# A two-layer adaLN kernel: the results of the last mixture of experts gathered one step ahead, their sums placed by hand on VectorE

## The chip, the cores and the metric

One core of one Trainium2 chip runs the whole kernel. The metric is the device time of one execution in microseconds (us); the time of a kernel is the median of its runs. A profile is one further execution, recorded instruction by instruction.

The engines are named as the profile names them: PE is the matrix engine (TensorE), DVE is VectorE, ACT is ScalarE, POOL is GpSimd, and SP only issues transfers. Each engine works through its own queue in order. An instruction that waits holds up everything queued behind it on its engine.

## The reference, cut to what matters

The kernel computes two transformer-like layers on 4096 tokens of width 128. Only the end of the second layer is touched: a mixture of eight experts with a top-2 choice, a capacity of 512 slots for each expert, and a residual sum.

```python
def _dispatch_compute(xf, top_expert, w1, w2, capacity):
    ...
    xe = jnp.where(valid[..., None], xf[tok_idx], 0.0)
    h = jax.nn.gelu(jnp.einsum('ech,ehf->ecf', xe, w1), approximate=True)
    ye = jnp.einsum('ecf,efh->ech', h, w2)
    ...
    out = jnp.zeros((tokens + 1, hs), xf.dtype).at[tok_safe.reshape(-1)].add(ye.reshape(-1, hs))
    return out[:tokens]
...
for k in range(TOP_K):
    y = _dispatch_compute(xf, top_experts[:, k].astype(jnp.int32), w1, w2, capacity)
    out = out + y * expert_weights[:, k][:, None]
return out.reshape(sl, bs, hs) + bias
...
x = x + gb * _L1_ffn_ref(h, L1_ffn_router_w, L1_ffn_w1, L1_ffn_w2, L1_ffn_bias)
```

There are 4096 tokens in this stage, so the capacity is 4096 / 8 = 512 slots for each expert and choice. What matters here is its last part: each token's two expert results are fetched, multiplied by a weight and by the gate `gb`, and added to `x`.

## The kernel before

The kernel is one program whose instructions are written in Python loops and then ordered by a planner. The planner simulates the engines while it places instructions: of the instructions that it takes to be ready it issues the one that was traced first, so the order on an engine can differ from the order of the text. `tc.keep_in_program_order(ins)` adds an edge that holds `ins` behind the last instruction traced on its engine before it; it is an order of issue and not a wait.

The end of the kernel has three stages.

**The slots stage.** `slots_steps` (L1312) runs over the two choices `k` and the eight experts `e`, 16 experts in all. `expert(k, e)` loads 512 rows of the expert's inputs (`xe`), transposes them on PE (`xtp`), copies them from PSUM on DVE (`xT`, L1272) and multiplies them with the first weights (`ph`, 8 matmul instructions) into ACT's gelu (`act`, L1278). `expert_out` (L1281) multiplies with the second weights (`ypy`, 32 instructions), copies the result on DVE (`ye`, L1290) and stores it from ACT's queue to `slots_out` in HBM (L1291). `expert_out` of one expert is traced after `expert` of the next. `outs` gives `ypy` two PSUM buffers; `xtp` has one.

**The gathers.** `collect(k, g)` (L1293) handles four tiles of 128 tokens. For each tile, POOL issues an indirect transfer (L1297) that gathers 128 rows of `slots_out` by an index list into a tile `y` (a ring of 8 buffers); DVE multiplies `y` by weight and gate (L1305) and adds it to `x` (L1308). 28 of the 32 tiles go this way, in 7 groups of four. For `k` = 0 the groups are traced in the slots stage, group `e` in the step of expert (1, `e`). A gather of choice `k` reads all of `slots_out[k]`, so it can start only when all eight experts' results of that choice have been stored. For `k` = 1 the groups are traced in the next stage, and SP stores each finished group (L1310).

**The blocks stage.** The last 512 tokens were sorted into 15 blocks of 128 rows with one expert each. `last_experts` (L1092) goes over them in pairs: `hidden(j)` does the first multiplication (`gph`) and the gelu (`gact`), at every second pair also the transpose (`gtp`) and DVE's copy of it (`gxT`, L1118); `results(j)` does the second multiplication (`gpy`, one PSUM buffer), DVE's product with the gate (`gye`, L1139), the next weights' loads on SP and a store to `g_out`. `results` of a pair is traced after `hidden` of the next pair. `Beside.take(1)` runs the generator by one pair. For each group `g` the loop takes one pair and then traces `collect(1, g)`; the eighth pair and the last `results` follow behind the seventh group.

**The tail.** `return_steps` gathers the last 512 tokens' rows from `g_out` (8 gathers `fy`, L287), adds them and stores.

Of the kernel before, what the change touches and what calls it, by code (L numbers as in the profile page):

```python
# [14 lines left out]
ALU = mybir.AluOpType  # L15
# [5 lines left out]
NT = B * S // P  # L21
TB = S // P
# [18 lines left out]
NL = TB // 2  # L41
# [3 lines left out]
def mm(nc, out, lhsT, rhs, start=True, stop=True):  # L45
    return nc.tensor.matmul(out, lhsT, rhs, start=start, stop=stop)  # L46
# [3 lines left out]
def adaln_two_layers(ctx: ExitStack, tc: tile.TileContext, I: dict, out: bass.AP):  # L50
    nc = tc.nc
# [43 lines left out]
    with tc.tile_pool(name="mw", bufs=1) as mw, tc.tile_pool(name="mps", bufs=2, space=PSUM) as mps:  # L95
        for l in range(2):
# [23 lines left out]
            for m in (2, 5):  # L120
# [7 lines left out]
                g = cst.tile([P, B, D], F32, name=f"gate{l}{m}")  # L128
                nc.vector.scalar_tensor_tensor(g, raw, -1.0, size, ALU.add, ALU.mult)
                gate.append(g)  # L130
    gate_a0, gate_b0, gate_a1, gate_b1 = gate
# [130 lines left out]
    def load_block(pool, bufs, tag, table, expert, j):  # L262

        w = pool.tile([P, I[table].shape[2]], F32, tag=tag, bufs=bufs, name=tag)

        with tc.issue_after(loads[-1].ins) if loads else nullcontext():
            e = nc.sync.value_load(expert[0:1, j : j + 1], min_val=0, max_val=NE - 1)
            loads.append(nc.sync.dma_start(w.unsqueeze(1), I[table][bass.ds(e, 1)].rearrange("e p c -> p e c")))
        return w
# [193 lines left out]
    with ExitStack() as es:  # L463
# [192 lines left out]
        blocks = None  # L656
# [4 lines left out]
        for at, (b, c) in enumerate(stages):  # L661
            q, k = made
# [45 lines left out]
            blocks = None  # L708
            if c == 0 and b > 0:
                blocks = Blocks(b - 1, ab, (ps_m, "m"), [(ps_m, "m")], rest)  # L710
# [20 lines left out]
    wgt = w1l.tile([P, 2, NT], F32, name="wgt")  # L731
# [5 lines left out]
    with ExitStack() as es:  # L737
# [354 lines left out]
        def last_experts():  # L1092

            b, nb = B - 1, NLB
            expert = sent[0][0]
            rows_in = g_in.rearrange("(q p) d -> p q d", p=P)
            rows_out = g_out.rearrange("(q p) d -> p q d", p=P)
            ws, ins, xT, ye = {}, {}, {}, {}

            def load(j):  # L1100
                for r in range(j, min(j + 2, nb)):
                    ws[r] = load_block(eb, 6, "gw", "g_w", expert, r)

            def rows(q):
                n = min(4, nb - q)
                ins[q] = eb.tile([P, 4, D], F32, tag="gxe", name="gxe")
                nc.sync.dma_start(ins[q][:, :n], rows_in[:, q : q + n])

            def hidden(j):
                q = j - j % 4  # L1110
                if j == q:
                    n = min(4, nb - q)
                    tp = ps_m.tile([P, 4, P], F32, tag="m", name="gtp")
                    for r in range(n):
                        nc.tensor.transpose(tp[:, r], ins[q][:, r], ident)
                    xT[q] = eb.tile([P, 4, P], F32, tag="gxT", name="gxT")
                    shift, scale = modT[1][:, 3, b : b + 1], modT[1][:, 4, b : b + 1]
                    nc.vector.tensor_scalar(xT[q][:, :n], tp[:, :n], scale, shift, ALU.mult, ALU.add)  # L1118
                    if q + 4 < nb:
                        rows(q + 4)  # L1120
                    ye[q] = eb.tile([P, 4, D], F32, tag="gye", name="gye")
                n = min(2, nb - j)
                ph = [ps_u.tile([P, NFC, P], F32, tag=f"pu{(j + r) % 4}", name="gph") for r in range(n)]
                act = eb.tile([P, 2, NFC, P], F32, tag="gact", name="gact")
                for r in range(n):
                    for f in range(NFC):
                        mm(nc, ph[r][:, f], ws[j + r][:, f * P : (f + 1) * P], xT[q][:, j - q + r])
                    nc.scalar.activation(act[:, r], ph[r], AF.Gelu_apprx_tanh)
                return j, n, act

            def results(j, n, act):
                q = j - j % 4
                py = ps_y.tile([P, 2, D], F32, tag="py", name="gpy")
                for r in range(n):
                    w = ws.pop(j + r)
                    for f in range(NFC):
                        w2 = w[:, NFC * P + f * D : NFC * P + (f + 1) * D]
                        mm(nc, py[:, r], act[:, r, f], w2, start=(f == 0), stop=(f == NFC - 1))
                nc.vector.tensor_mul(  # L1139
                    ye[q][:, j - q : j - q + n], py[:, :n], gate_b1[:, b : b + 1, :].to_broadcast([P, n, D])  # L1140
                )
                if j + 6 < nb:
                    load(j + 6)
                if j > q or j + n == nb:
                    nc.scalar.dma_start(rows_out[:, q : j + n], ye[q][:, : j + n - q])

            rows(0)
            for j in range(0, 6, 2):
                load(j)
            made = None  # L1150
            for j in range(0, nb, 2):
                ahead = hidden(j)
                if made is not None:
                    results(*made)
                made = ahead
                yield
            results(*made)
# [26 lines left out]
        for b in range(B):  # L1184
# [17 lines left out]
            for m in range(NCH):  # L1202

                g, n = divmod(m, NCH // 2)
# [56 lines left out]
        def expert(k, e):  # L1261
            at = slice(e * CAP, (e + 1) * CAP)
            xe = eb.tile([P, NS, D], F32, tag="xe", bufs=4, name="xe")
            load_xe = nc.sync.dma_start(xe, xd[k][at, :].rearrange("(q p) d -> p q d", p=P))
            if (k, e) == (1, NE - 1):

                loads.append(load_xe)
            tp = ps_m.tile([P, CAP], F32, tag="m", name="xtp")
            for q in range(NS):
                nc.tensor.transpose(tp[:, q * P : (q + 1) * P], xe[:, q, :], ident)  # L1270
            xT = eb.tile([P, CAP], F32, tag="xT", name="xT")
            nc.vector.tensor_copy(xT, tp)  # L1272
            act = eb.tile([P, NFC, CAP], F32, tag="act", name="act")
            for f in range(NFC):
                pool, tag = next(banks)
                ph = pool.tile([P, CAP], F32, tag=tag, name="ph")
                mm(nc, ph, g_w[:, e, f * P : (f + 1) * P], xT)
                nc.scalar.activation(act[:, f, :], ph, AF.Gelu_apprx_tanh)  # L1278
            return e, k, act

        def expert_out(e, k, act):  # L1281
            at = slice(e * CAP, (e + 1) * CAP)
            pool, tag = next(outs)
            py = pool.tile([P, NS, D], F32, tag=tag, name="ypy")
            for q in range(NS):
                for f in range(NFC):
                    w = g_w[:, e, NFC * P + f * D : NFC * P + (f + 1) * D]
                    mm(nc, py[:, q, :], act[:, f, q * P : (q + 1) * P], w, start=(f == 0), stop=(f == NFC - 1))
            ye = eb.tile([P, NS, D], F32, tag="ye", name="ye")
            nc.vector.tensor_copy(ye, py)  # L1290
            nc.scalar.dma_start(yd[k][at, :].rearrange("(q p) d -> p q d", p=P), ye)  # L1291

        def collect(k, g):  # L1293

            for t in range(4 * g, 4 * g + 4):
                y = eb.tile([P, D], F32, tag="y", bufs=8, name="y")
                nc.gpsimd.indirect_dma_start(  # L1297
                    out=y,
                    out_offset=None,
                    in_=yd[k][:, :],  # L1300
                    in_offset=bass.IndirectOffsetOnAxis(ap=slot[:, k, t : t + 1], axis=0),
                    bounds_check=NSLOT - 1,
                    oob_is_err=False,
                )
                nc.vector.scalar_tensor_tensor(  # L1305
                    y, y, wgt[:, k, t : t + 1], gate_b1[:, t // TB, :], ALU.mult, ALU.mult
                )
                nc.vector.tensor_add(x[:, t, :], x[:, t, :], y)  # L1308
            if k == 1:
                nc.sync.dma_start(outv[:, 4 * g : 4 * g + 4, :], x[:, 4 * g : 4 * g + 4, :])  # L1310

        def slots_steps():  # L1312
            waiting = None
            for k in range(2):
                for e in range(NE):
                    made = expert(k, e)
                    yield
                    if waiting is not None:
                        expert_out(*waiting)
                    waiting = made  # L1320
                    if k == 1 and 4 * e < NT - NL:
                        collect(0, e)
                    yield
            expert_out(*waiting)

# [4 lines left out]
            sending.take(sending.n)  # L1330
        slots.rest()
        blocks = Beside(last_experts(), 0, 1)
        for g in range((NT - NL) // 4):
            blocks.take(1)
            collect(1, g)
        blocks.rest()
        _, placei, w = sent[0]
        drained(return_steps(g_out, NT - NL, NL, placei, w, db, 6, store=True))
# [73 lines left out]
```

## Time and profile before

| | us |
|---|---|
| median of 3 runs | 2165.16 (2164.11 to 2168.03) |
| the profiled execution's own time | 2174.76 |
| its span, first to last instruction | 2173.1 |
| slots stage's second half, experts (1, 1) on: first `ph` | 2004.01 |
| first gather of choice 0 | 2007.76 |
| blocks stage: first `gph` | 2091.13 |
| first gather of choice 1 | 2095.02 |
| first gather of the tail | 2158.26 |

Busy shares over the whole span: PE 82%, DVE 61%, POOL 46%, ACT 44%. In the stretch from 2004 to 2057 us PE was busy 29.93 of 53 us, and from 2095 to 2158 us 31.63 of 63 us. The 56 gathers took POOL 994 to 1528 ns each, 996 in the median.

How to read the lines that follow in the prediction: a line of the timeline has the start in us, the busy time, the engine, the line of the kernel, the operation, the output and inputs, the shapes and the count; in brackets stands how long the engine sat idle before it and what ended that. A line of the waits has who waited, for whom, the total in us, the number of times and the longest. "remote" or "an unknown queue" means that the record doesn't tell what ended the wait. A line of the chain has the start, the length and the work or wait that the end hung on.

### The profile page before, as it was taken

How to read it: one execution, taken by the hardware profiler on the slowest of the kernel's cores; microseconds unless marked ns; L12 is line 12 of the kernel's file. 1: busy time of each engine (PE TensorE's matmuls, PEld its weight loads, DVE VectorE, ACT ScalarE, POOL GpSimd, SP SyncE). 2: the span in 40 equal slices, each digit the busy share in tenths (PEclk: the TensorE clock that was granted, in tenths of full speed). 3: DMA queues.
4: the chain of work that ended last, by engine and by line, in shares of the span. 5: the costliest groups of instructions: out<-in, count | busy, mean ns of one | idle time of the engine just before them, and what ended most of it. 6: DMA issues, size and time to landing. Idle time of an engine off the chain costs nothing. (4 is left out here: it accounts for less than half of the span.)

```text
span 2173.1 us, 29054 instructions
## 1 busy us (share of the span) xinstructions
PE 1790.6 (82%) x8957; PEld 967.9 (45%) x8957; DVE 1322.2 (61%) x4000; ACT 948.1 (44%) x2073; POOL 997.5 (46%) x1277
## 2 busy tenths in 40 slices
PE   5399999998999999899988899958688777659573
PEld 3144444454555344455534455523245323237363
DVE  5446566665667667566766566647678796941322
ACT  1145454653445375354365345544465354323111
POOL 1334534336423635532544533345563867740433
PEclk9699999999999999999999999988799877869786
DMA  6400101001222201222300122110122400012334
GB/s 224 128 1 19 31 1 34 16 19 45 67 71 70 64 1 41 66 69 64 83 13 24 51 71 66 52 37 0 36 65 79 144 9 20 15 60 82 115 94 127
DMA packets 103756, 123.59 MB, mean 57 GB/s; under 512 B 15024, under 2 KB 68656, under 8 KB 103600
## 3 DMA queue, kind: packets, MB, share of 16 engines
q1 hardware_dynamic: 84256, 99.01, 15.6%
q0 software_dynamic: 8192, 16.74, 2.6%
q10 hardware_dynamic: 11152, 5.97, 0.9%
q8 instruction: 71, 1.16, 0.2%
q14 instruction: 85, 0.70, 0.1%
HBM read 67.85 MB, written 32.90 MB: 46 GB/s over the span
## 5 line engine op out<-in xcount | busy, mean ns | idle before, releaser
L586 POOL TENSOR_SCALAR pr<-pr,den 128x32 f32<-128x32 f32 (+31 forms) x512 | 354.6, 709 | 303.4 <-DVE den L583 297.2
L580 ACT ACTIVATE pr<-pr,nb 128x32 f32<-128x32 f32 (+31 forms) x512 | 371.6, 727 | 197.3 <-DVE nb L567 193.0
L595 PE MATMUL pt<-ident,pr 128*128 128x128 f32 x2304 | 341.8, 283 | 47.1 <-POOL pr L586 37.6
L46 PE MATMUL sc<-k,q 64*128 64x512 f32 (+14 forms) x1536 | 332.7, 525 | 44.4 <-DVE nb L567 25.3
L595 PEld LDWEIGHTS pt<-ident,pr 128*128 128x128 f32 x2304 | 253.5, 142 | 244.0 <-POOL pr L586 78.8
L46 PE MATMUL po<-pT,v 128*64 128x512 f32 x1152 | 345.4, 621 | 1.9 <-DVE pT L599 1.5
L597 ACT COPY pT<-pt 128x512 f32<-128x512 f32 x288 | 167.8, 583 | 362.5 <-PE pt L595 297.7
L567 DVE CUSTOM_DVE_ANT_0 pr<-sc,mask 128x512 f32<-128x512 f32 (+15 forms) x512 | 273.0, 559 | 73.5 <-PE sc L46 64.1
L599 DVE COPY pT<-pt 128x512 f32<-128x512 f32 x288 | 198.3, 688 | 167.3 <-PE pt L595 153.7
L46 PEld LDWEIGHTS sc<-k,q 64*128 64x128 f32 x1536 | 123.8, 193 | 199.9 <-DVE nb L567 94.7
L914 POOL TENSOR_TENSOR hc<-h,cc 128x512 f32<-128x512 f32 x128 | 161.9, 1278 | 102.1 <-DVE h L910 37.7
L46 PE MATMUL pu<-du,spread 128*128 128x512 f32 x256 | 147.0, 679 | 48.8 <-DVE h L910 41.7
L684 POOL MEMSET pr<- 128x288 f32 x128 | 42.4, 340 | 262.8 <-PE pt L595 258.8
L567 DVE CUSTOM_DVE_ANT_0 pr<-sc,mask,nb 128x416 f32<-128x416 f32 (+15 forms) x256 | 119.9, 496 | 6.9 <-PE sc L46 5.8
L908 ACT ACTIVATE da<-dt,negA 128x512 f32<-128x512 f32 x128 | 91.6, 719 | 65.5 <-DVE h L910 65.1
L1297 POOL DMA_INDIRECT y<-slots_out,slot x56 | 56.9, 1016 | 126.6 <-issue 59.2
L46 PEld LDWEIGHTS po<-pT,v 128*64 128x64 f32 x1152 | 69.4, 135 | 84.9 <-issue 44.5
L503 DVE TENSOR_TENSOR rot_w<-proj,sin_sb 128x512 f32<-128x512 f32 x80 | 55.0, 688 | 79.8 <-PE proj L46 45.9
L906 DVE TENSOR_TENSOR pu<-pu,bb 128x512 f32<-128x512 f32 x128 | 85.1, 684 | 23.8 <-PE pu L46 23.3
L46 PEld LDWEIGHTS pu<-du,spread 128*128 128x128 f32 x256 | 45.8, 208 | 117.8 <-DVE h L910 70.5
L545 POOL TENSOR_TENSOR q<-rot_u,rot_v 128x512 f32<-128x512 f32 x64 | 81.3, 1272 | 35.1 <-DMA rot_v<-rot_w 26.2
L580 ACT ACTIVATION_READ_ACCUMULATOR pr<-pr,nb 128x1 f32 x512 | 96.3, 188 | 0.0
(273 smaller groups left out, 2708.9 us busy)
## 6 DMA issues: line engine op xcount, KB each, us to landing
fw<-in_f_w SPq DMA_DIRECT2D x92, 320.0 KB
rot_v<-rot_w SPq DMA_DIRECT2D x320, 64.0 KB
gw<-in_g_w SPq DMA_DIRECT2D x15, 512.0 KB
fxe<-blocks_in SPq DMA_DIRECT2D x28, 192.0 KB
blocks_out<-fye SPq DMA_DIRECT2D x28, 192.0 KB
blocks_in<-mask SPq DMA_DIRECT2D x20, 256.0 KB
slots_in<-mask SPq DMA_DIRECT2D x16, 256.0 KB
g_w<-in_g_w SPq DMA_DIRECT2D x8, 512.0 KB
```

Of the source, the lines that this page charges most:

```text
L46: return nc.tensor.matmul(out, lhsT, rhs, start=start, stop=stop)
L545: nc.gpsimd.tensor_add(to, u.rearrange("p (n q) -> p n q", q=QG), v.rearrange("p (n q) -> p n q", q=QG))
L567: nc.vector.tensor_tensor_reduce(out=pr[hp][:, g, lo:hi], in0=sc[:, hp, : hi - lo], in1=mask[:, MW - hi + lo :] if hi == nk else mask[:, : ...
L580: nc.scalar.activation(p, p, AF.Exp, bias=nb[:, last, hp : hp + 1], scale=-1.0, accum_out=den[:, hp : hp + 1])
L586: nc.gpsimd.tensor_scalar(p, p, den[:, hp : hp + 1], 1.0, ALU.mult, ALU.mult)
L595: next_to(hp == 0 and g == 0, lambda: nc.tensor.transpose(to, p, ident))
L597: nc.scalar.copy(pT[:, hp, :], pt)
L599: nc.vector.tensor_copy(pT[:, hp, :], pt)
L906: nc.vector.tensor_mul(pu, pu, bb[:, tok])
L908: nc.scalar.activation(da, dt[:, tok], AF.Exp, scale=negA[:, c : c + 1])
L914: nc.gpsimd.tensor_mul(hcs[-1], h, cc[:, tok])
L1297: nc.gpsimd.indirect_dma_start(out=y, out_offset=None, in_=yd[k][:, :], in_offset=bass.IndirectOffsetOnAxis(ap=slot[:, k, t : t + 1], axis=0),
```

## The change

`collect` is split in two. `fetch(k, g)` only issues the four gathers and keeps the tiles in a list `came`; `add_oldest()` takes the oldest group out of the list and traces its products and sums, and for choice 1 the store. Each product (not the sum behind it) is held behind the instruction traced last on DVE.

In the slots stage nothing is traced in the step of expert (1, 0). From expert (1, 1) on, each step traces the sums of the group that an earlier step fetched, and then fetches group `e - 1`. So group 0 is fetched in step 1 and added in step 2, and group 6 is fetched in step 7 and added in the blocks stage. In the blocks stage each step adds the group fetched a step before, fetches the next and takes a pair; the last group is added after the eighth pair.

```diff
-        def collect(k, g):
-
+        came = []
+
+        def fetch(k, g):
+
+            here = []
             for t in range(4 * g, 4 * g + 4):
                 y = eb.tile([P, D], F32, tag="y", bufs=8, name="y")
                 nc.gpsimd.indirect_dma_start(
...
-                nc.vector.scalar_tensor_tensor(
-                    y, y, wgt[:, k, t : t + 1], gate_b1[:, t // TB, :], ALU.mult, ALU.mult
+                here.append((t, y))
+            came.append((k, g, here))
+
+        def add_oldest():
+
+            if not came:
+                return
+            k, g, here = came.pop(0)
+            for t, y in here:
+
+                tc.keep_in_program_order(
+                    nc.vector.scalar_tensor_tensor(
+                        y, y, wgt[:, k, t : t + 1], gate_b1[:, t // TB, :], ALU.mult, ALU.mult
+                    )
                 )
                 nc.vector.tensor_add(x[:, t, :], x[:, t, :], y)
...
-                    if k == 1 and 4 * e < NT - NL:
-                        collect(0, e)
+
+                    if k == 1 and e > 0:
+                        add_oldest()
+                        fetch(0, e - 1)
                     yield
...
         blocks = Beside(last_experts(), 0, 1)
+        blocks.take(1)
         for g in range((NT - NL) // 4):
+            add_oldest()
+            fetch(1, g)
             blocks.take(1)
-            collect(1, g)
+        add_oldest()
         blocks.rest()
```

## The prediction

> **What bounds the kernel now.** I read the chain that ended last from 2000 us on, then the waits, then the timeline, then the busy time by stretch. In the slots stage PE should be the bound: in an undisturbed step the first multiplication, the second and a transpose follow each other without a gap, and the starts of `ph` stand 7.55 us apart (2057.29 and 2064.84). From the second expert of choice 1 on this breaks:
>
> ```profile
> 2004.01 3.69 PE L46 MATMUL ph<-xT,g_w 128*128 128x512 f32 x8
> ...
> 2007.76 1.04 POOL L1297 DMA_INDIRECT y<-slots_out,slot  x1 [49.72 <-PE ph L46]
> ...
> 2010.46 0.35 DVE L1305 SCALAR_TENSOR_TENSOR y<-y,wgt,gate 128x128 f32<-128x128 f32 x1 [6.52 <-DMA y<-slots_out,slot]
> ...
> 2014.64 0.68 DVE L1290 COPY ye<-ypy 128x512 f32<-128x512 f32 x1
> ...
> 2020.38 0.68 DVE L1272 COPY xT<-xtp 128x512 f32<-128x512 f32 x1
> 2021.12 6.04 PE L46 MATMUL ph<-xT,g_w 128*128 128x512 f32 x8 [7.40 <-DVE x L1308]
> ...
> 2032.16 0.60 ACT L1278 ACTIVATE act<-ph 128x512 f32<-128x512 f32 x1 [23.83 <-remote]
> ...
> 2043.42 0.69 DVE L1290 COPY ye<-ypy 128x512 f32<-128x512 f32 x1 [10.23 <-remote]
> ...
> 2057.29 3.70 PE L46 MATMUL ph<-xT,g_w 128*128 128x512 f32 x8 [2.30 <-DVE xT L1272]
> ...
> 2064.84 3.69 PE L46 MATMUL ph<-xT,g_w 128*128 128x512 f32 x8
> ```
>
> The reader is to see that the transpose for `xT` was done by 2010.6, yet DVE copied it at 2020.38, because the planner put eight products of gathered tiles (the first at 2010.46, the eighth at 2019.71) and their sums ahead of it and the gathers arrive only every 1.30 us (25 gathers between 2007.76 and 2039.12). PE starves behind that copy. The second gap is of another kind: `ph` was issued by 2027.16, but ACT saw it only at 2032.16, and DVE saw `ypy` at 2043.42. In that time POOL issued gathers back to back until 2040.12, then stopped for want of `y` buffers. Three steps, from 2004.01 to 2057.29, took 53.28 us where 3 x 7.55 = 22.65 are work: **30.6 us are lost** here. The waits of 2008 to 2090 us say the same:
>
> ```profile
> ACT act L1278 <- remote: 33.1, 3, 23.8
> ...
> DVE y L1305 <- DMA y<-slots_out,slot: 23.4, 17, 6.5
> ```
>
> The blocks stage shows both again. Its gathers start at 2095.02, and the tail's first gather follows at 2158.26, 63.2 us later. Between them PE is busy 31.63 us. The chain has this stretch in it, while 27 gathers run from 2095.02 to 2130.07:
>
> ```profile
> 2112.24 0.42 DVE gye L1139
> 2112.66 0.27 DVE y L1305
> 2112.93 0.13 ACTq L1145
> 2113.06 20.22 another core or an unknown queue
> 2133.32 0.04 issue
> 2133.36 0.61 ACT gact L1128
> 2134.01 3.78 PE gpy L46 x16
> ```
>
> PE had issued the `gph` that this `gact` needs by 2113.93. So whatever PE finishes under a long run of gathers reaches ACT and DVE late, up to some 3 us after the run ends (2130.07 to 2133.36; 2040.12 to 2042.64).
>
> **The change part by part.** No instruction is added or removed: 56 gathers of 1.0 us, 56 products of 0.35 and 56 sums of 0.28 us stay, as do the stores.
>
> *The fetch of choice 0 a step later.* It costs nothing, since the first gather waits for the store of expert (0, 7): it comes at 2007.76, already in the step of expert (1, 1), to which the change moves it. If that store came 7 us earlier, the step would cost up to 7.55 us of gather time, still covered by the slots stage. On POOL only gathers stand behind it.
>
> *The sums of choice 0 two steps later.* Group 0 is now behind `ye` of expert (1, 1), which comes one step of 7.55 after 2010.2, at about 2017.7. Its fourth gather starts at 2011.72 and lands after some 2.5 us, at 2014.3. DVE doesn't wait. Groups 0 and 1 fill the 8 buffers by 2018.2; group 2 starts when group 0 is added (about 2019), has landed by 2027 and is added behind `ye` of (1, 3) at 2033 or later. So POOL issues 8 gathers and then fours with pauses. This frees the 30.6 us. Against it stands what is new ahead of `xT`: the sums are traced before the next expert's copy. Four products and sums in a row take 1.85 us (pairs of tiles start 0.925 us apart, 2044.83, 2045.75, 2046.68). Six such groups lie in the stage: 0 us if PE has `ypy` of the next expert to do meanwhile (it ran 18 of those ahead at 2011 to 2013.7), 11 us if not. I take 4, nearer to the first, since 3.5 us of `ypy` are at hand in each step. Then PE's late results under short runs of gathers. In the run of six at 731 us ACT waited 3.0 and 3.2 us for PE's transposes, in the one at 1077 us 4.6; in those at 746 and 1092 us it went on as soon as PE had ended. Bounds are 0 and 7 x 4.6 = 32 us; I take 5, one such wait of 4.6 us and little else, since most of the seven groups now come as runs of four, and the one such run of gathers in the record (1725 us) shows none. So the slots stage gains 30.6 - 4 - 5 = **22 us** (range 30.6 - 11 - 32 = -12 to 30.6).
>
> *The weights for the blocks.* SP loads them (six of 512 KB) after the last `xe`, at 2045.26 before; they move forward with it, into the time of groups 1 and 2. There a gather took 6.21 us to land while they ran (2049.05). Group 2 would land at 2030.5 instead of 2027, still ahead of 2033: nothing. Without that slack it is 3.5 us once.
>
> *The sums of choice 1 a step later.* Call S the first gather of choice 1. It follows the last `ye` by 5.4 us as before. POOL needs 28 x 1.30 = 36.4 us, and PE some 29 us in all, so gathers set the pace. Group g is added behind `gye` of pair g. With no late result the last sum ends at S + 36.4 + 3; `gye` of the last pair and its store (2155.24 to 2158.26: 3.0 us) give the tail's first gather at S + 42.5, **20.7 us** earlier than the S + 63.2 of now. The other end: each run of gathers holds PE's results until 3.2 us after it. Then eight gathers cost 10.4 + 3.2, and each of the next five fours 5.2 + 3.2 + 1.0 of `gact` and `gye`: 13.6 + 47 + two last pairs of 3 us = S + 67, 4 us later than now. A run can't grow to 27 any more, because the sums that free its buffers are behind `gye`, which waits for PE. I take 11, a little above the middle, since short runs were harmless in two of four. What queues behind a waiting sum on DVE is `gye` and `gxT` of the next pair, and PE and ACT wait for those; the stores on SP move back one step, ahead of weights for pairs three steps on, which have slack of two steps.
>
> [...]
>
> **The sum.** 22 + 11 = 33 us off the profiled 2174.76 (span 2173.1 and 1.66 around it) gives 2141.8. The median of the runs shown is 9.6 below the profiled time, and I carry the difference over: 2165.2 - 33 = **2132**.
>
> **The rivals.**
>
> A. *All of it*: no late PE result and sums wholly covered, 30.6 + 20.7 = 51 us: 2114. For it, two of four short runs without a trace of lateness; against it, the runs at 731 and 1077.
>
> B. *The late results were the greater part and stay*: the slots stage gains only the 9.6 us that DVE's own queue cost (2011.55 to 2021.12), the blocks stage loses 4: 2160. For it, the 33.1 us of unknown waits of ACT; against it, that they arose in runs of 25 and 27.
>
> C. *Slower: every group's run of gathers freezes PE.* In the slots stage seven runs each hold PE's increments for 6.2 us (3.0 + 3.2, the run at 731 us) ahead of ACT's gelu: 43.4 us against 30.6 freed, and 4 lost in the blocks stage: 2165 + 13 + 4 = 2182. It decides from 30.6 / 7 = 4.4 us a run. Against it, 746 and 1092.
>
> [...]
>
> E. *The change doesn't do what it says*: the planner already had another order in which DVE waits as before; 2165. Against it, the pin leaves no such order for the products.
>
> **How the numbers follow.** Forecast 0.56 (2122 to 2144 by its own bounds), A 0.12, B 0.13, C 0.10, D 0.05, E 0.04. A measurement of this kernel tells 0.2%, 4.3 us, from no change. Faster: forecast, A, B, D = 0.86; same: E = 0.04; slower: C = 0.10. The range leaves out C, E and the edges: 2112 to 2162.
>
> **What would show it.** In the changed profile no product of choice 0 waits for a gather; the starts of `ph` of experts (1, 1) to (1, 7) stand 7.5 to 9.5 us apart; `ye` is followed by four products and sums, then `xT`; gathers of choice 0 come as eight, then fours; ACT's waits by "remote" in the slots stage fall from 33.1 to under 8 us. S is near 2073, the tail's first gather at S + 50 to 54. I am wrong if ACT still waits more than 4 us at each run of gathers, if DVE waits for `y` in the slots stage, or if S + 63 stays.

## The result, and the profile after

The changed kernel takes 2131.9 us in the median of 6 runs (2130.7 to 2139.1), the kernel before 2165.6 (6 runs, 2161.7 to 2169.4): a ratio of 0.985, 95% interval [0.983, 0.987]. The medians are 33.7 us apart; by the interval the gain is 28 to 36 us. The profiled execution took 2139.09 us with a span of 2137.4, 35.7 less than the span before.

The slots stage in the timeline of the changed kernel (columns as before):

```profile
2016.05 3.69 PE L46 MATMUL ph<-xT,g_w 128*128 128x512 f32 x8
...
2023.92 0.69 DVE L1290 COPY ye<-ypy 128x512 f32<-128x512 f32 x1 [7.93 <-PE xtp L1270]
2024.53 0.34 DVE L1319 SCALAR_TENSOR_TENSOR y<-y,wgt,gate 128x128 f32<-128x128 f32 x1
2024.79 0.69 DVE L1272 COPY xT<-xtp 128x512 f32<-128x512 f32 x1
2025.39 0.28 DVE L1323 TENSOR_TENSOR x<-x,y 128x128 f32<-128x128 f32 x1
...
2025.53 3.70 PE L46 MATMUL ph<-xT,g_w 128*128 128x512 f32 x8 [1.55 <-DVE xT L1272]
...
2025.94 0.99 POOL L1300 DMA_INDIRECT y<-slots_out,slot  x1 [3.31 <-DVE y L1319]
```

```profile
2033.28 3.70 PE L46 MATMUL ph<-xT,g_w 128*128 128x512 f32 x8
2040.99 3.70 PE L46 MATMUL ph<-xT,g_w 128*128 128x512 f32 x8
2048.56 3.70 PE L46 MATMUL ph<-xT,g_w 128*128 128x512 f32 x8
2056.14 3.70 PE L46 MATMUL ph<-xT,g_w 128*128 128x512 f32 x8
```

No product waits for its gather, and only one product comes ahead of `xT`: the sums are not pinned, so the planner put `xT` between the first product and its sum. One `ph` waits 1.55 us, those behind it follow at 7.6 to 7.8 us. That wait isn't made by the product ahead of `xT`. The `ypy` that `ye` copies had ended at 2022.20, and DVE began at 2023.92, 1.3 us after the run of eight gathers (2012.47 to 2022.64): it is a late result of PE, of 1.7 us, though the record names another releaser. The slots-only kernel below has the same order without this wait. From the first gather of choice 0 (2012.47) to that of choice 1 (2070.74) are 58.3 us; before it was 87.3.

The blocks stage in the same timeline, ACT, DVE's `gye` and POOL alone:

```profile
2085.12 1.00 POOL L1300 DMA_INDIRECT y<-slots_out,slot  x1 [0.30 <-issue]
2087.14 0.60 ACT L1128 ACTIVATE gact<-gph 128x512 f32<-128x512 f32 x1 [4.32 <-remote]
2087.89 0.42 DVE L1139 TENSOR_TENSOR gye<-gpy,gate 128x256 f32<-128x256 f32 x1 [8.49 <-remote]
...
2089.17 1.00 POOL L1300 DMA_INDIRECT y<-slots_out,slot  x1 [3.05 <-DVE y L1319]
...
2098.39 1.00 POOL L1300 DMA_INDIRECT y<-slots_out,slot  x1 [0.30 <-issue]
2099.55 0.60 ACT L1128 ACTIVATE gact<-gph 128x512 f32<-128x512 f32 x1 [9.64 <-remote]
...
2122.68 0.96 POOL L287 DMA_INDIRECT fy<-g_out,g_placei  x1 [10.04 <-DMA g_out<-gye]
```

Here PE's results are still seen late: these `gact` and `gye` start only when a run of 12 gathers, and then one of 8, has ended. In the waits of this stage (2066 to 2124 us) the same stands as sums:

```profile
ACT gact L1128 <- remote: 17.5, 4, 9.6
DVE gye L1139 <- remote: 16.7, 3, 8.5
```

From the first gather of choice 1 to the tail's first gather are 51.9 us; before it was 63.2. The two stages together gained 40.3 us. The span shows 35.7, because ahead of the change, where both programs are alike, this execution ran 4.7 us later (first gather of choice 0 at 2012.47 against 2007.76).

### The profile page after: what moved, and what is told of

Read it like the earlier page. It is cut to its first block, busy times and chain, and to the rows that moved or that the text cites. A ratio compares the mean times of both kernels' runs of the same rounds, so it can differ in the third digit from the quotient of the medians.

```text
span 2137.4 us, 29054 instructions
## 1 busy us (share of the span) xinstructions
PE 1792.8 (84%) x8957; PEld 971.7 (45%) x8957; DVE 1323.7 (62%) x4000; ACT 947.3 (44%) x2073; POOL 994.6 (47%) x1277
## 3 DMA queue, kind: packets, MB, share of 16 engines
q1 hardware_dynamic: 84256, 99.01, 15.7%
## 5 line engine op out<-in xcount | busy, mean ns | idle before, releaser
L595 PE MATMUL pt<-ident,pr 128*128 128x128 f32 x2304 | 341.9, 283 | 46.4 <-POOL pr L586 37.0
```

Source lines behind the costliest of these rows:

```text
L595: next_to(hp == 0 and g == 0, lambda: nc.tensor.transpose(to, p, ident))
```

## The experiments

There were five comparisons, each on one chip and beside the kernel before; the table goes by them. "Slots" is the time from the first gather of choice 0 to that of choice 1, "blocks" from there to the tail's first gather, both from the profile; "remote" is the sum of waits by "remote" of ACT and DVE from 1995 us on. Ratios are to the kernel before on the same chip, with 95% intervals. Gains in the text are worked out from the ratio and its interval, so they can differ by up to 2 us from the difference of the medians.

A wait counts from the end of the waiting engine's last work. The sums by "remote" therefore hold time in which PE was still at work too, and a late result can stand under another releaser's name, as in the step above: they show where to look, and not what was lost. The changed kernel itself ran in the first and the third comparison only, both on chips with late results; on a chip without them only its parts and its variants ran.

| kernel | before there, us | this, us | ratio | slots | blocks | remote |
|---|---|---|---|---|---|---|
| before, first profile | 2165.6 | | | 87.3 | 63.2 | 81.1 |
| after, first profile | 2165.6 | 2131.9 | 0.985 [0.983, 0.987] | 58.3 | 51.9 | 34.2 |
| pin only | 2155.2 | 2133.4 | 0.991 [0.989, 0.992] | 64.3 | 45.7 | 0 |
| ahead only | 2155.2 | 2158.5 | 1.002 [1.0005, 1.003] | 78.1 | 55.3 | 0 |
| slots only | 2155.2 | 2137.4 | 0.992 [0.990, 0.993] | 56.6 | 53.6 | 0 |
| blocks only | 2155.2 | 2145.8 | 0.996 [0.994, 0.997] | 77.9 | 42.7 | 0 |
| before again | 2169.5 | 2168.2 | one run | 81.4 | 61.4 | 37.3 |
| after again | 2169.5 | 2133.4 | 0.984 [0.983, 0.985] | 58.5 | 51.1 | 27.8 |
| blocks two ahead | 2169.5 | 2130.0 | 0.983 [0.981, 0.985] | 58.3 | 48.9 | 32.9 |
| 16 buffers | 2169.5 | 2153.3 | 0.993 [0.992, 0.995] | 68.8 | 57.8 | 80.1 |
| 4 buffers | 2154.7 | 2129.3 | 0.989 [0.987, 0.992] | 56.7 | 46.4 | 0 |
| plain, POOL | 2154.7 | 2116.9 | 0.984 [0.981, 0.987] | | | 0 |
| plain, SP | 2154.7 | 2120.2 | 0.985 [0.983, 0.987] | | | 0 |
| plain, POOL, again | 2170.5 | 2113.8 | 0.973 [0.970, 0.976] | | | 0 |

The theory: two losses lay in each stage. DVE's order (products and sums that wait for gathers stand ahead of the copies that PE needs) is taken away by the change. That PE's late results depend on how long the runs of gathers are is my estimate; the runs show it on one chip alone (waits by "remote" of 80.1 us with 16 buffers, 27.8 with 8).

### One part at a time

**Pin only.** Against the changed kernel, the fetch goes back to the step of its own sums:

```diff
-                    if k == 1 and e > 0:
+                    if k == 1 and 4 * e < NT - NL:
+                        fetch(0, e)
                         add_oldest()
-                        fetch(0, e - 1)
...
-        blocks.take(1)
         for g in range((NT - NL) // 4):
-            add_oldest()
-            fetch(1, g)
             blocks.take(1)
-        add_oldest()
+            fetch(1, g)
+            add_oldest()
```

> One part alone: the products are pinned in the order in which they are traced, but a group is fetched and added in the step of the kernel before, the fetch just ahead of its own sums. If what cost the 30 us was that the planner gathered eight and twelve products together ahead of xT, and kept POOL in one run of 25 gathers, the pin alone takes most of it: groups of four, each of which DVE waits for some 4.5 us (first gather to its landing 2.5 us, the fourth 3.9 us later), so about 2140 to 2150. Rival: with no step between fetch and sums, DVE stands in front of xT and ye in each of seven steps for the 6 to 7 us of four gathers and their landing, 7 x 6.5 = 45 us against 30 freed in the slots stage and about as before in the blocks stage: 2165 to 2180.

The pin alone takes 20.3 us (16 to 24), more than expected. The timeline of this kernel in the step of expert (1, 1) and the next:

```profile
2004.15 0.36 DVE L1319 SCALAR_TENSOR_TENSOR y<-y,wgt,gate 128x128 f32<-128x128 f32 x1 [6.56 <-DMA y<-slots_out,slot]
...
2009.66 0.68 DVE L1272 COPY xT<-xtp 128x512 f32<-128x512 f32 x1
...
2010.39 6.59 PE L46 MATMUL ph<-xT,g_w 128*128 128x512 f32 x8 [4.59 <-DVE xT L1272]
...
2019.81 1.04 POOL L1300 DMA_INDIRECT y<-slots_out,slot  x1 [0.30 <-DVE ye L1290]
...
2020.64 3.70 PE L46 MATMUL ph<-xT,g_w 128*128 128x512 f32 x8
```

DVE waits for the first group and PE with it, 4.59 us and a slow `ph`. It happens once and not seven times, which is where the rival fails: POOL's queue runs ahead of the trace as far as the 8 buffers let it (20 gathers back to back, the last at 2026.46), so from the second group on the gathers are ahead by themselves. The step between fetch and sums is worth the first group: 64.3 against 56.6 us in the slots-only kernel. In the blocks stage it is 45.7 against 42.7 us in the blocks-only kernel.

**Ahead only.** The other part, the products not pinned:

```diff
-                tc.keep_in_program_order(
-                    nc.vector.scalar_tensor_tensor(
-                        y, y, wgt[:, k, t : t + 1], gate_b1[:, t // TB, :], ALU.mult, ALU.mult
-                    )
+                nc.vector.scalar_tensor_tensor(
+                    y, y, wgt[:, k, t : t + 1], gate_b1[:, t // TB, :], ALU.mult, ALU.mult
                 )
```

> The other part alone: fetches and sums stand where the changed kernel has them, but the products are not pinned, so the planner may take them ahead of traced work. If the pin is what gives the gain, the products of choice 0 stand again in front of ye and xT while their gathers are still under way, the slots stage keeps most of its loss of 29 us and the time is 2155 to 2170. Rival: the step between fetch and sums suffices whatever the planner does, and the time is within 5 us of 2132.

It gains nothing; it is 3.7 us slower (1 to 6.5). Its timeline:

```profile
2020.09 5.25 PE L46 MATMUL ph<-xT,g_w 128*128 128x512 f32 x8 [4.37 <-DVE xT L1272]
...
2039.85 0.35 DVE L1318 SCALAR_TENSOR_TENSOR y<-y,wgt,gate 128x128 f32<-128x128 f32 x1 [1.20 <-DMA y<-slots_out,slot]
...
2040.92 0.68 DVE L1272 COPY xT<-xtp 128x512 f32<-128x512 f32 x1
...
2041.65 6.41 PE L46 MATMUL ph<-xT,g_w 128*128 128x512 f32 x8 [12.09 <-DVE xT L1272]
```

The planner again puts products that still wait for gathers ahead of `ye` and `xT`, and PE waits 12.09 us. So the pin is the part without which nothing is won; by the profiles the other part adds to it.

**Slots only** keeps the change for choice 0 and has choice 1 as before, unpinned; **blocks only** keeps it for choice 1 and has choice 0 as before, unpinned. Against the changed kernel, slots only (with `product` the name of the unpinned product):

```diff
+                if k == 0:
+                    tc.keep_in_program_order(product)
...
-        blocks.take(1)
+        add_oldest()
         for g in range((NT - NL) // 4):
-            add_oldest()
-            fetch(1, g)
-            blocks.take(1)
-        add_oldest()
+            if g:
+                blocks.take(1)
+            fetch(1, g)
+            add_oldest()
```

and blocks only:

```diff
+                if k == 1:
+                    tc.keep_in_program_order(product)
...
-                    if k == 1 and e > 0:
+                    if k == 1 and 4 * e < NT - NL:
+                        fetch(0, e)
                         add_oldest()
-                        fetch(0, e - 1)
```

> The change in the slots stage alone (choice 0 fetched ahead and pinned), the blocks stage as in the kernel before. If the trace read right, 29.0 us of the gain lie here: 2165.6 - 29 = 2137, with first gather to first gather of choice 1 at 58 us and the blocks stage at 63. Rival: the two stages share one loss, because gathers of choice 0 that end earlier only move the same late results of PE into the blocks stage: then this kernel gains under 20 us, 2146 or more.

> The change in the blocks stage alone (choice 1 added a step later and pinned), the slots stage as in the kernel before. If the trace read right, 11.3 us lie here: 2165.6 - 11 = 2154, with the first gather of choice 1 to the tail's first gather at about 52 us. Rival: what the blocks stage gained came with the shorter runs of gathers in the stage ahead of it; then this kernel is within 4 us of the kernel before.

Slots only gains 17.7 us (14 to 21), not 29, and blocks only 9.7 (6.5 to 13). The rival of a loss shared between the stages does not explain the first figure either: the kernel before is 10 us faster on this chip, and no wait by "remote" stands in any of the four profiles. What is left is DVE's order alone. The blocks-only kernel, whose slots stage has the order of before, shows it:

```profile
2010.07 3.69 PE L46 MATMUL ph<-xT,g_w 128*128 128x512 f32 x8
...
2027.15 6.37 PE L46 MATMUL ph<-xT,g_w 128*128 128x512 f32 x8 [7.37 <-DVE xT L1272]
...
2041.86 5.85 PE L46 MATMUL ph<-xT,g_w 128*128 128x512 f32 x8 [6.34 <-DVE xT L1272]
...
2053.79 1.55 PE L46 MATMUL ph<-xT,g_w 128*128 128x512 f32 x3 [2.08 <-DVE xT L1272]
```

PE waits 7.37 + 6.34 + 2.08 = 15.8 us for `xT`, and two `ph` after such a wait take 2.7 and 2.2 us longer than 3.69: 20.7 of the 21.3 us between 77.9 and the 56.6 of the slots-only kernel. By the times this part is worth 17.7 us (14 to 21), somewhat less than by this one pair of profiles.

The slots-only kernel has DVE's and PE's order of the changed kernel in the slots stage, instruction for instruction. The step in which the changed kernel's `ph` waited 1.55 us reads here:

```profile
2012.88 0.69 DVE L1290 COPY ye<-ypy 128x512 f32<-128x512 f32 x1 [6.25 <-PE ypy L46]
...
2014.49 3.70 PE L46 MATMUL ph<-xT,g_w 128*128 128x512 f32 x8
```

`ye` follows its `ypy` (ended at 2012.85) at once, and `ph` doesn't wait: it starts 7.79 us after the one before it, against 9.48 in the changed kernel. So the 1.55 us there came from the late result and not from the sums. In the slots-only kernel's blocks stage, unpinned, the same:

```profile
2088.48 0.35 DVE L1318 SCALAR_TENSOR_TENSOR y<-y,wgt,gate 128x128 f32<-128x128 f32 x1 [3.94 <-DMA y<-slots_out,slot]
...
2090.37 0.42 DVE L1139 TENSOR_TENSOR gye<-gpy,gate 128x256 f32<-128x256 f32 x1
...
2090.93 2.05 PE L46 MATMUL gpy<-gw,gact 128*128 128x128 f32 x8 [10.42 <-DVE gye L1139]
```

PE waits 10.42 us for a `gye` that stands behind products that wait for gathers. Pinned, the stage takes 42.7 instead of 53.6 us.

### Late results: the chip, the run, the kind of transfer

**Both kernels again**, on another chip.

> The kernel before once more, for a profile beside those of the parts, in none of which ACT or DVE waited by 'remote'. If the late results of PE belong to the chip or the execution and not to the program, this profile shows none either: first gather to first gather of choice 1 about 78 us (the stage of the blocks-only kernel, which runs the same order) and not 87.3, from there to the tail's first gather about 54 (slots-only kernel) and not 63.2. Rival: they belong to this program's order, and 87 and 63 come back.

> The changed kernel once more, for its ratio beside the parts'. Slots-only gave 0.9918 and blocks-only 0.9955; if the parts add up, 0.987 to 0.988, 27 us. If they take in more together, it is the 0.985 of the first comparison. Without late results its blocks stage lasts 43 to 46 us (the blocks-only and pin-only kernels had 42.7 and 45.7), with them 52 as in its first profile.

Here the late results are back, in other places than the first time: the waits of the kernel before say

```profile
ACT gact L1128 <- remote: 36.7, 2, 28.2
```

and its slots stage is 81.4 us, with no long "remote" in it; neither the 78 nor the 87 of the two expectations. It has a late result all the same, under another name:

```profile
2036.13 5.83 PE L46 MATMUL ph<-xT,g_w 128*128 128x512 f32 x8 [5.88 <-DVE xT L1272]
...
2048.72 1.57 ACT L1278 ACTIVATE act<-ph 128x512 f32<-128x512 f32 x3 [19.83 <-PE ypy L46]
```

The four parts of this `ph` were ready from 2038.20 to 2041.96, and ACT took the first at 2048.72, 2.8 us after a run of 28 gathers (2008.93 to 2045.96). Earlier in the same run ACT had gone on at once, from 2024.52 to 2028.28.

As far as five comparisons tell, late results come with the chip. In the seven profiles of the two comparisons in which the kernel before took 2155 us, one increment of PE's (the record of the signal that an instruction of PE has ended) comes more than 0.6 us behind the end of its instruction (by 2.1 us); in the six profiles of the first and this comparison there are 42 to 56 in each, from 500 us on. Not all of these are delays. The six records hold 2049 to 2065 increments, the other seven 2096 or 2097, and where one is missing, the next one's time stands for it, though the engine that needed it may have gone on at once. A delay is shown only where the engine itself starts late. Nor is it an effect of the profiler: the kernel before has medians of 2154.7 and 2155.2 us without late results and of 2165.6 to 2170.5 with them. On this chip the change is worth 34.7 us (32 to 38); whether the parts add up can't be read from it, since they ran on the other kind of chip.

**16 buffers**, against the changed kernel:

```diff
-                y = eb.tile([P, D], F32, tag="y", bufs=8, name="y")
+                y = eb.tile([P, D], F32, tag="y", bufs=16, name="y")
```

> The changed kernel with 16 buffers for y in place of 8, so that no gather waits for a buffer. If the length of a run of gathers is what makes PE's results late, the blocks stage, one run of 28 now, becomes longer again by some 5 to 10 us and the waits by 'remote' come back. If buffers are what breaks the run at 12 and 20 gathers in the changed kernel's first profile (3.1 and 2.7 us of pause), and there are no late results on this chip, it is 0 to 5 us faster than the changed kernel; if POOL's pace is already whole there, the same within 2 us.

On the same chip 2153.3 against 2133.4: twice the buffers cost 20 us by the medians. The profiled executions are 15.7 us apart, and their two stages 17 us (68.8 + 57.8 against 58.5 + 51.1). The blocks stage is 6.7 us longer, as expected of late results; the 10.3 us in the slots stage I had not expected. The slots stage's timeline:

```profile
2016.09 1.00 POOL L1300 DMA_INDIRECT y<-slots_out,slot  x1 [0.30 <-issue]
2016.79 0.69 DVE L1290 COPY ye<-ypy 128x512 f32<-128x512 f32 x1 [12.72 <-remote]
...
2025.44 1.00 POOL L1300 DMA_INDIRECT y<-slots_out,slot  x1 [0.30 <-issue]
...
2028.92 1.58 ACT L1278 ACTIVATE act<-ph 128x512 f32<-128x512 f32 x3 [20.47 <-remote]
...
2031.56 1.00 POOL L1300 DMA_INDIRECT y<-slots_out,slot  x1 [5.12 <-DVE y L1319]
```

Where the changed kernel stops after 8 gathers, POOL goes on for 20, until 2026.4. `ye` comes at 2016.79 (its `ypy` had ended at about 2012), and ACT sees `ph` at 2028.92, 2.5 us after the run. Neither DVE's order nor the gathers' place in the trace differ from the changed kernel. So on this chip the longer run of gathers came with later results. Length alone doesn't set it, since ACT went on at once for much of the run of 28 above.

**Blocks two ahead**, a version that might beat both: the changed kernel with

```diff
         blocks = Beside(last_experts(), 0, 1)
-        blocks.take(1)
+        blocks.take(2)
```

> A version that may beat both: the changed kernel with the blocks of the last experts traced one step further ahead of the sums of choice 1. In the blocks-only kernel the tail's first gather starts 6.2 us after POOL's last gather of choice 1 has ended, for it waits for the store of the last gye, which stands behind the sums of group 5. Here that gye stands behind group 4, 5.2 us of gathers earlier. If POOL sets the pace of the blocks stage, the tail starts right behind the last gather and 5 to 6 us are won against the changed kernel. Rival: PE sets the pace (29 us of work that starts ahead of the gathers, and waits behind DVE), so the last gye is no earlier and the time is that of the changed kernel.

Against the changed kernel on the same chip the medians are 3.5 us apart and the intervals overlap, so it can't be told from it. Its timeline shows why it didn't win 5 to 6 us here:

```profile
2103.30 1.00 POOL L1300 DMA_INDIRECT y<-slots_out,slot  x1 [0.31 <-DVE x L1323]
2105.48 0.60 ACT L1128 ACTIVATE gact<-gph 128x512 f32<-128x512 f32 x1 [7.42 <-remote]
2108.24 0.29 DVE L1139 TENSOR_TENSOR gye<-gpy,gate 128x128 f32<-128x128 f32 x1 [4.29 <-PE gpy L46]
2111.29 0.96 POOL L287 DMA_INDIRECT fy<-g_out,g_placei  x1 [7.00 <-DMA g_out<-gye]
```

The last `gye` no longer stands behind a group's sums, but its `gact` saw PE only after the last gather. On a chip without late results it wasn't tried.

**4 buffers** (`bufs=4` in the same line).

> The changed kernel with 4 buffers for y in place of 8: POOL can issue no more than four gathers before it waits for the sums. If the length of a run is what makes PE's results late, no wait by 'remote' over 3 us is left. But the fetch is no longer ahead: from the first gather of a group to its last sum are 3.9 us of issue, 2.5 of landing and some 1 us of sums, behind a gye or ye of the step; seven groups of choice 1 take 7 x 8 to 9 = 56 to 63 us, against 51 in the changed kernel, so 2137 to 2146 where the changed kernel has 2133. Rival: only the total of gathers in a stage counts, the late results stay, and the blocks stage becomes 65 us or longer: 2148 or more.

This chip showed no late results, so the run tells nothing of them. It does show that the price which I expected is not there: the blocks stage takes 46.4 us, not 56 to 63, because POOL pauses only 0.4 to 2 us at a time; the sums follow each gather's landing and free one buffer at a time. The changed kernel wasn't run on this chip, so 4 and 8 buffers can't be compared by time.

**Plain transfers** in place of the gathers, with 16 buffers. These kernels leave the gather by index out, so the rows come in the order in which they are stored:

```diff
-                nc.gpsimd.indirect_dma_start(
-                    out=y,
-                    out_offset=None,
-                    in_=yd[k][:, :],
-                    in_offset=bass.IndirectOffsetOnAxis(ap=slot[:, k, t : t + 1], axis=0),
...
+                nc.gpsimd.dma_start(y, yd[k][t * P : (t + 1) * P, :])
```

and, for the second, `nc.sync.dma_start` with the same operands.

> The kernel with 16 buffers for y, in which POOL fetches each tile by a plain transfer of 128 rows that lie together instead of a gather by index: the gather by index is left out, so the rows come in the order in which they are stored. Same queue engine, same bytes, same buffers, same waits. If issuing gathers by index on POOL (1.0 us each, back to back) is what makes PE's results late, the waits by 'remote' of the two stages (80 us in the kernel with 16 buffers on the chip before) fall under 8 us and the time falls by 20 us or more against that kernel, to 2135 or less. Rival: the bytes landing in SBUF, or any transfer that POOL issues, make them late; the waits stay at 40 us or more and the time at 2145 or more. Only on a chip where the kernel before takes 2165 or more does this tell the two apart; where it takes 2155, no late results are to be seen in any kernel.

> The same plain transfers of rows that lie together (the gather by index is left out), issued by SP instead of POOL; 16 buffers for y. If POOL's issuing is the cause, no wait by 'remote' is left, and the blocks stage is no longer paced by POOL's 1.30 us a gather but by PE's 29 us: first fetch of choice 1 to the tail's first gather under 42 us, time under 2125. Rival: the landing of 64 KB tiles itself is the cause, then ACT and DVE wait for PE's results here too, 20 us or more in the two stages.

Both ran on a chip without late results, as the kernel before at 2154.7 shows, so they said nothing of the cause. From the start of the last `ph` to the tail's first gather they take 47.3 and 46.9 us, against 58.1 in the blocks-only kernel, some 11 us less, also where nothing is late. I put this down to gathers that wait for all eight stores and then go one by one; the 16 buffers instead of 8 were not tried apart from it. The first was run once more:

> The kernel of 16 buffers with plain transfers on POOL (the gather by index is left out) once more, since the first time no kernel of that chip showed late results. If this chip shows them (kernel before at 2165 or more, as with the 16-buffer kernel of gathers at 2153 and 80 us of waits by 'remote'): should gathers by index be the cause, waits by 'remote' in the two stages are under 8 us and the time under 2125; should any transfers of POOL or the landing of the tiles be, 40 us or more and 2140 or more. If the kernel before takes 2155, the question stays open.

This time the chip was one with late results (the kernel before at 2170.5). The groups of the fetches, the waits of the whole span, and the timeline at 733 us, where this program still gathers by index:

```profile
L1300 POOL DMA_DIRECT2D y<-slots_out x56: 534/534/587, 1956.7 to 2079.9; - x56
```

```profile
ACT pT L597 <- remote: 3.2, 1, 3.2
```

```profile
733.60 0.95 POOL L287 DMA_INDIRECT fy<-blocks_out,f_placei  x1 [0.30 <-issue]
734.43 0.58 ACT L597 COPY pT<-pt 128x512 f32<-128x512 f32 x1 [3.23 <-remote]
```

30 increments of PE's stand late in the record of this execution, all before 1961 us; none in the two stages. At 734.43 ACT begins 1.6 us behind the end of the transposes that it copies (732.80); in this kernel's first run, on the chip without late results, it was 0.1 us (733.81 against 733.73). The median of 2113.8 us is no longer than the 2116.9 of that chip. So in these two stages the late results went with the gathers by index: with plain transfers on the same engine's queue, of the same bytes, they are gone, on a chip on which the kernel before takes 2170.5. Two things changed together, though. A plain transfer of rows that lie together needs only one expert's store and takes POOL 0.53 us, so the fetches start earlier and come in fours, never in a long run. Whether a long run of plain transfers would do the same was not tried.

## Why the prediction was right, and where not

The forecast, 2132, was met by the median of 2131.9. By its own steps:

**What bounds the kernel.** Right: DVE's order and PE's late results, in both stages. Their shares were open in the prediction, and the chips without late results give them, by one profile of each kernel and across chips. Of the 30.6 us lost in the slots stage 21.3 were DVE's order with the slow `ph` behind it (77.9 against 56.6), and up to 9.4 were late results (87.3 against 77.9). The slow `ph`, 4.9 of the 21.3 us, had no term of its own in the prediction, though its line at 2021.12 shows 6.04 us. Of the 20.7 us between 63.2 and the ideal of 42.5 in the blocks stage, 10.9 were DVE's order (53.6 against 42.7) and 9.6 late results.

**The fetch of choice 0 a step later, the weights moving forward:** nothing, as said; no `ph` and no product waits for either in the slots stage.

**The sums of choice 0:** forecast 22 us, measured 29.0 (87.3 to 58.3). Both terms set against the 30.6 were too large. The 4 us of sums ahead of `xT` were 0.3: in the slots-only kernel the starts of `ph` of experts (1, 1) to (1, 7) span 45.6 us, where six steps of 7.55 are 45.3. Only one product comes ahead of `xT`, since the pin holds the products and leaves the sums to the planner. The 5 us of late results were 1.7, once, at the end of the run of eight; behind the fours ACT and DVE went on at once. The 5 us were too large because waits had been read as lateness. The two waits at 731 us, 3.0 and 3.2 us, are 3.01 and 2.05 us in the blocks-only kernel on a chip without late results (at 735.14 and 737.78), so 1.2 of the 6.2 us were lateness; of the 4.6 us at 1077 it was 2.7 (the transposes ended at 1083.35, ACT began at 1086.01).

**The sums of choice 1:** forecast 11 us, measured 11.3. The ideal of S + 42.5, with S the first gather of choice 1, was right (42.7 us in the blocks-only kernel, where nothing is late). That 11 and 11.3 agree is in part luck, for the 11 came from another split than I argued. I took the whole 20.7 for late results of which about half would go; in fact half was DVE's order, all of which went, and half late results, which stayed (51.9 against 42.7). Nor did the gathers come as eight and then fours in this stage, as the other end of that estimate assumed, but as 12, 8 and 8.

**The sum.** 40.3 us in the two stages, where I had 33. The two that make the median come out all the same are the base and the drift. I carried the 9.6 us between profiled execution and median over as if they lay elsewhere; but the second profile of the kernel before has 142.8 us in the two stages where the first had 150.5, so of the two the first was the execution that lost more in these stages. The second pair of profiles gives 142.8 - 109.6 = 33.2 us, the size of the forecast. The profile that I worked from held some 8 us more loss than this second one, and my terms took out some 7 us too little: that the two cancel in the median is luck.

**The rivals.** A (all of it, 2114) fails on the late results of the blocks stage. B (late results the greater part, and they stay) was right for half of the blocks stage and wrong in the slots stage: DVE's queue cost 21, not 9.6, since the second gap, which I put down to late results, is there without them too (6.34 us of waiting for `xT` in the blocks-only kernel, whose slots stage has the same order). C would need 4.4 us lost at each run; it was 1.7 us once, behind the run of eight, and nothing behind the fours. D, that sums on DVE hold gathers on POOL for the 1.85 us of a group: no run shows such a price. In the changed kernel the gathers beside the sums take 997 ns in the median and 1075 at most, those beside none 997 and 1038, so sums don't hold them there; in the kernel before one of the 36 beside sums took 1.53 us (at 2139.97), and their median is 1.00. E fails: the pin does what it says, and without it the planner does restore DVE's waits.

**What would show it.** Held: no product of choice 0 waits; `ph` at 7.5 to 9.5 us; gathers as eight, then fours; "remote" in the slots stage from 33.1 to 0, though the one late result there stands under another name; the tail's first gather at S + 51.9. Not held: `ye` is followed by one product, not by four products and sums, and then by `xT`; S was 2070.7 and not 2073.

## What to carry to other kernels

Where a planner takes whatever is ready by its own model, an operation that waits for an unevenly late transfer (in the kernel before DVE took one gather's tile 2.7 us after the gather had started, at 2010.46, and another's 6.2 us after, at 2055.28) has to be pinned behind the work that others need; fetching earlier in the text did nothing without the pin, because the planner put the waiting products ahead again. With the pin it was worth one group, because the queue already ran ahead as far as its buffers allowed. A ring of buffers is also a throttle: on a chip with late results 16 buffers instead of 8 lost 20 us. A wait is not yet a delay: compare the start of the waiting engine with the end of the work that it needs. And one profile is one execution on one chip: take a second before the difference between profile and median is carried over.

## What the runs showed of the hardware

*Late results of PE.* In three of five comparisons, while POOL issued gathers by index back to back (1.00 us each, one every 1.30 us), ACT and DVE went on up to 21 us behind the end of PE's work (`gact` at 2133.36 for a matmul that ended at 2112.45 in the first profile of the kernel before). Some did so while the run still went on (2032.16 there), others 0.2 to 3.3 us after its end. In the changed kernel's slots stage DVE began 1.7 us late behind the run of eight. In the fours behind it, with pauses of 2 to 3 us between them, neither ACT nor DVE waited: the record has an increment 3.6 us behind its instruction there, but the engine had gone on without it, at 2062.11 for a `ypy` that ended at 2062.07. What carries the delay was not found.

*PE slow after a wait.* In the busy time by stretch of the blocks-only kernel (columns: start and end, length, then busy time and count of PE, PE's weight loads, DVE, ACT, POOL, then PE's granted clock, the DMA share and GB/s), the stretch before the first long wait for `xT` and those that hold the two slow `ph`:

```profile
2004.00:2014.00 10.00, 10.00 (x54) 6.87 (x53) 1.29 (x2) 4.13 (x8) 0.05 (x1) 1.00 0.27 77
...
2027.00:2031.00 4.00, 3.85 (x5) 1.79 (x6) 1.51 (x7) 0.63 (x2) 3.04 (x4) 0.50 0.20 49
...
2041.00:2046.00 5.00, 4.14 (x5) 1.85 (x6) 2.17 (x8) 0.92 (x2) 3.78 (x5) 0.50 1.01 352
```

After 7.37 and 6.34 us without work PE runs at a granted clock of 0.50, and eight matmuls take 6.37 and 5.85 us instead of 3.69. So the stall of 7.37 us cost 10.1 and that of 6.34 us cost 8.5; behind the wait of 2.08 us `ph` took 3.70 us as ever, at a granted clock of 1.00 (2053 to 2060 us). So in this trace the two long waits brought a clock of 0.50, and the short one did not.
